# A pre-norm graph network: the hand-over between layers in another order, and one norm named later

## The chip, the cores and the metric

The program runs on one core of a Trainium2 chip, in one launch. The metric is the device time of that core in microseconds (us). A core has a matrix engine (TensorE, PE; weight loads are listed as PEld), VectorE (DVE), ScalarE (ACT), GpSimd (POOL) and SyncE (SP), which issues most DMAs. Each engine works through its own queue in order and waits on semaphores for the others.

## What is computed

```python
mu, var = jnp.mean(x, 0), jnp.var(x, 0)          # x: relu of a layernorm of the input
h = (x - mu) * rsqrt(var + EPS) * bn_w + bn_b
h = _gcn(h, src, dst, gcn_in_w, gcn_in_b, n)
for i in range(L):
    a = _attn(_ln(h, ln2_w[i], ln2_b[i]), cond, Wq[i], Wk[i], Wv[i], Wo[i])
    h = h + a
    u = _ln(h, ln3_w[i], ln3_b[i]) @ geglu_w[i] + geglu_b[i]
    val, gate = jnp.split(u, 2, axis=-1)
    f = val * jax.nn.gelu(gate, approximate=False)
    h = h + f @ ffo_w[i] + ffo_b[i]
h = _gcn(h, src, dst, gcn_out_w, gcn_out_b, n)
```

There are N = 1024 rows of D = 512, L = 4 layers, 8 heads of 64. `_gcn` multiplies by a weight and sums over 16384 edges. `_attn` is cross attention: 16 batches of 64 rows look at 256 rows of `cond` each, with k = cond @ Wk and v = cond @ Wv. All is float32.

## The kernel before

The rows `h` stay in SBUF as eight blocks of 128 (`h[0]` to `h[7]`, views of `hall`). Attention runs over eight groups g, one for each block of 128 rows (two batches). While group g is weighted, k and v of group g + 1 are made.

k and v are made with float32 products of higher precision than one pass gives: each operand is split into three parts. `left_parts` splits a group's condition `ct` into `ah` (ACT), `al` (DVE) and `as` (POOL, from `ah` and `al`); `right_parts` splits a weight into `bh` (ACT), `bl` and `bs` (DVE). A `Twelve` is one 128x512 block of k or v: `begin` multiplies the first two pairs of parts (two groups of four matmuls) and has ACT scale the bank in place; `end` adds the third pair (one group) and copies the bank out, on ACT or DVE by the flag `by`. `staggered` runs a list of such units so that a unit's `end` comes after the next one's `begin`, and runs other work `beside` a unit.

Weights are multiplied in seven products instead of eight (a Strassen form), hence names such as `wqs`, `ln2S` (sums of blocks), and `ffn_out` with products 0, 6, 4, 5, 1, 3, 2 into the four banks `fa` to `fd`; DVE adds them to `kept` and `hall`. `ffn_out(l, r, s, ...)` does half s of the rows (blocks 0, 1, 4, 5 or 2, 3, 6, 7). Its argument `beside` holds up to three functions: the third is called after the first add of `kept`, the first after the three shared adds, the second after the add of product 1.

What sets the order: the engine queues are filled by a planner that simulates the program and issues, on each engine, whatever is ready and was named first. `pin` keeps an instruction behind everything named before it on its engine, `in_order(engine)` does that for a whole block, `issue_after` and `waiting_for` hold instructions behind a given one. Most matmuls are pinned. Tiles come from pools: `slots` has 36 slots of 128x1024 floats, from which weights, parts, `kT`, `v` and `lnT` all come; `work` has ten tiles of 128x512 (`xn`, `pr`, `pT`, `oT` and others); PSUM has eight banks.

The hand-over from layer l to l + 1 is the end of the loop over layers, in one block with DVE in written order. It names the loads of Wk, condition 0, Wv, Wq, the bias row and condition 1 (`load_projections`), then: the first half of the last `ffn_out`, with Wk's split beside it; the moments of blocks 0, 1, 4, 5; the second half, with, in this order, those blocks' root and norm on ACT (`ready_first`, `scaled_by_act`), condition's parts (`split_cond`) and Wv's parts; the moments, root and norm of the other four blocks. The next layer begins with `keys` and `values` of group 0, eight units, with `turn_first` (transposes of the normalised blocks into `lnT`, scaled by ACT and DVE) beside unit 4 and unit 7; then the queries.

In group 6 (`NG - 2`) the norm of blocks 4 and 5 (`ln3_norm`: moments and root as small operations on 128x2, and two scalings, all on DVE) is named ahead of group 7's keys, and POOL makes the sums of the geglu weights (`geglu_weights`, held behind the scores). `mix` transposes the probabilities, copies them (`pT`, on ACT and DVE in turn), and weights v with them (bank `po`). The output projection of two groups at a time is a generator, `attn_out_pair`, whose last step is one product and its adds.

Of the kernel before, what the change touches and what calls it, by code (L numbers as in the profile page):

```python
# [8 lines left out]
F32 = mybir.dt.float32  # L9
# [16 lines left out]
def gnn_kernel(  # L26
# [85 lines left out]
    def t512(name, dtype=F32):  # L112
        return work.tile([P, 512], dtype, tag="t512", name=name)
# [27 lines left out]
    def rsqrt(var, name, eps=0.0):  # L141


        k = var.shape[1]

        def t(n, dtype=F32):
            return small.tile([P, k], dtype, tag=f"rs_{n}{k}", name=f"{n}_{name}",
                              bufs=4 if k == 1 else 2)

        v = t("v")  # L150
        rsqrt.first = nc.vector.tensor_scalar(v, var, float(eps), None, OP.add)
        y = t("y")
        nc.vector.tensor_scalar(y.bitcast(I32), v.bitcast(I32), -0.5, RSQRT_SEED, OP.mult, OP.add)
        for i in range(3):
            a = t("a")
            nc.vector.scalar_tensor_tensor(a, y, -0.5, v, OP.mult, OP.mult)
# [14 lines left out]
    def deviations(mv, name):  # L171

        return rsqrt(mv.rearrange("p (n c) -> p n c", c=2)[:, :, 1], name, EPS)
# [100 lines left out]
    def load_cond(l, g):  # L274
        if g < NG:
            raw_x[l, g] = slots_of(2, f"ct_{l}_{g}")
            for k in range(2):
                nc.sync.dma_start(raw_x[l, g][k].rearrange("p a b -> p (a b)"),
                                  cond_dram[g][:, 1024 * k:1024 * (k + 1)])
# [72 lines left out]
    class Twelve:  # L352
# [22 lines left out]
        def end(self):  # L375
            self.multiply(2, False, True)
            if self.by:
                nc.vector.tensor_copy(self.to, self.bank)
            else:
                nc.scalar.copy(self.to, self.bank)  # L380

    def staggered(units, beside):

# [14 lines left out]
    def values(l, g, wv, begun=None, n=0):  # L398

        vs[g] = begun or slots_of(2, f"v_{l}_{g}")  # L400
        return [Twelve(f"v_{l}_{g}_{c}", conds[g], c, wv, vs[g][c // 2][:, c % 2, :], c % 2)
                for c in range(n, 2 * MB)]

    kTs, vs = {}, {}
# [107 lines left out]
    bst = small.tile([P, KC, 2, 6], F32, tag="bst", name="bst", bufs=1)  # L512
# [817 lines left out]
    def scaled_by_act(blocks, mv, root, name):  # L1330

        n = len(blocks)
        less = small.tile([P, 4], F32, tag="less", name=f"less_{name}", bufs=1)[:, :n]
        scaled_by_act.last = nc.vector.scalar_tensor_tensor(less, mv.rearrange("p (n c) -> p n c", c=2)[:, :, 0], -1.0,
                                       root, OP.mult, OP.mult)
        for i, nb in enumerate(blocks):
            xns[nb] = t512(f"xn_{name}_{nb}")
            nc.scalar.activation(xns[nb], h[nb], AF.Identity, bias=less[:, i:i + 1],
                                 scale=root[:, i:i + 1])

    mv_ready = {}

    def take_moments(l, blocks):
        n = len(blocks)
# [24 lines left out]
    def four_wide(name):  # L1369
        return wos.tile([P, 4, 512], F32, tag="wos", name=name)  # L1370


    def load_projections(l):
        raw = [load_w(Wk[l], f"wk_{l}")]
        load_cond(l, 0)
        raw.append(load_w(Wv[l], f"wv_{l}"))
        raw.append(load_w(Wq[l], f"wq_{l}"))
        raw.append(load_row(ffo_b, l * D, f"ffb_{l}"))
        load_cond(l, 1)
        return raw  # L1380

    def load_last():
        w = load_w(gcn_out_w, "w_out")
# [18 lines left out]
            nc.sync.dma_start(c_dram[:, :, d, :].rearrange("s p n -> p s n"), by_sources(C[d]))  # L1402
    for l in range(L):

        lnS = ln_sums(l)
        if l:
            units = keys(l, 0, wk) + values(l, 0, wv)
            to_turn = [0, 1, 4, 5], [2, 3, 6, 7]
        else:
            scale_first(1, deviations(mv_first[1], "ln2_0_4"))  # L1410
            with waiting_for(scale_first.last, mybir.EngineType.Pool):
                wq = weight_sums(wq, "wqs_0")
            units = keys(0, 0, wk, begun["k0"], 2) + values(0, 0, wv, begun["v0"], 1)
# [74 lines left out]
        def scale_kept():  # L1488

            root = deviations(mv_kept, f"ln3_{l}_0")  # L1490
            scaled_by_act(range(4), mv_kept, root, f"ln3_{l}")

        def nothing():
            pass
# [2 lines left out]
        for g in range(NG - 1):  # L1497
# [4 lines left out]
            for end in ends:  # L1502
                end()
            if g == NG - 2:
                ln3_norm(g - 2, g - 1)
            if g == NG - 2:
                with waiting_for(scores.last, mybir.EngineType.Pool):
                    left = geglu_weights(l, 0, *raw)
            if not g:
# [1 line left out]
                    wo7 = wo_sums(wo)  # L1511
            if g in (1, 2):
                fetch_x(2 * l + g - 1)
            k = keys(l, g + 1, wk, *((begun["k1"], 1) if l == 0 and g == 0 else ()))
            for i, u in enumerate(k):
                u.begin()
                if i > 1:
# [186 lines left out]
        if last:  # L1704
            w_out, base, again, dinv_row = load_last()
            with waiting_for(Gated.last, mybir.EngineType.Pool):
                w_out = out_weights(nc.gpsimd, L, 0, w_out)
            ffn_out(l, R - 1, 0, fT, wff, kept)
        else:
            lnT = [slots_of(2, f"ln2T_{l + 1}_{i}") for i in range(2)]  # L1710
            raw_wk, raw_wv, wq, ffb = load_projections(l + 1)
            wk, wv = [[], [], []], [[], [], []]

            def split(to, raw, name, *of):
                for i in of:
                    for part, t in zip(to, right_parts(raw[i:i + 1], f"{name}_{l + 1}_{i}")):
                        part.extend(t)
# [157 lines left out]
```

## Time and profile before

| what | value |
|---|---|
| time, median of 3 runs | 2452.02 us (2450.74 to 2453.26) |
| the profiled execution | 2452.32 us, span 2450.5 us |
| busy: PE, PEld | 97%, 73% |
| busy: DVE, ACT, POOL | 66%, 41%, 38% |
| mean granted TensorE clock | 0.994 |

The span is the time from the first to the last instruction; the rest of the execution's time lies around it. Busy shares are means over stages of different kinds: where PE is busy for nearly the whole of a stage, the other engines' idle time there costs nothing, so the list of PE's waits and the stages in which they lie say more. A row of the timeline reads: start, duration, engine, line, operation, output from inputs, shapes, how many merged, and in brackets the idle time before it and what ended it.

### The profile page before, as it was taken

To read this page: it belongs to the slowest core of one execution; us is meant where nothing else is said; L and a number is where in the kernel's file an instruction comes from. 1 tells how busy PE (TensorE), PEld (TensorE's weight loads), DVE (VectorE), ACT (ScalarE), POOL (GpSimd) and SP (SyncE) were. 2 spreads that over 40 slices of the span, in tenths; PEclk is the share of its full clock that TensorE was granted. 3 is DMA by queue.
4 is the path that set the end of the run, shared out by engine and by line. 5 is a ranking of instruction groups with operands and counts; after the bars stand their busy time and mean duration, and the time that the engine had idled before them with its cause. 6 is when DMAs were issued, how large, how long until landed. Compare 5 with 4: busy or idle time off the path is not lost. (4 is left out here: it accounts for less than half of the span.)

```text
span 2450.5 us, 33701 instructions
## 1 busy us (share of the span) xinstructions
PE 2374.2 (97%) x12528; PEld 1777.1 (73%) x12528; DVE 1606.8 (66%) x3028; ACT 992.8 (41%) x2011; POOL 937.2 (38%) x839
## 2 busy tenths in 40 slices
PE   8999999999999999999989999999999999999999
PEld 5668885677757886577776887577776887567787
DVE  9865456787764456877775445777785445678764
ACT  7444443343244444343334443533334444434320
POOL 0142233565133223565422223455523223356531
PEclk9999999999999999999999999999999999999999
DMA  6142110111301110021302101011121111011140
GB/s 197 37 133 83 64 57 18 44 43 52 108 26 66 39 48 23 22 61 47 116 1 65 65 19 52 9 52 52 43 91 48 48 53 35 18 45 42 52 146 35
DMA packets 108843, 138.31 MB, mean 56 GB/s; under 512 B 8232, under 2 KB 65904, under 8 KB 108672
## 3 DMA queue, kind: packets, MB, share of 16 engines
q1 hardware_dynamic: 106576, 130.64, 16.6%
q0 software_dynamic: 1376, 4.30, 0.5%
q8 instruction: 104, 1.70, 0.3%
q10 hardware_dynamic: 720, 1.11, 0.1%
q14 instruction: 67, 0.55, 0.1%
HBM read 119.25 MB, written 16.78 MB: 56 GB/s over the span
## 5 line engine op out<-in xcount | busy, mean ns | idle before, releaser
L316 POOL TENSOR_TENSOR as_c<-ah_c,al_c 128x512 fp32r<-128x512 f32 x128 | 189.4, 1507 | 243.4 <-DVE al_c L314 237.4
L1112 ACT ACTIVATE g<-g 128x512 f32<-128x512 f32 x192 | 112.1, 584 | 280.8 <-PE g L1098 278.5
L373 ACT ACTIVATE v<-v 128x512 f32<-128x512 f32 x127 | 74.0, 583 | 256.7 <-PE v L362 256.7
L1049 POOL TENSOR_TENSOR gsa<-gha,gla 128x512 fp32r<-128x512 f32 x96 | 125.7, 1331 | 104.2 <-DVE gla L1046 104.2
L362 PE MATMUL v<-bh_wv,ah_c 128*128 128x512 f32 x508 | 149.5, 417 | 5.7 <-ACT kT L380 5.7
L1049 POOL TENSOR_TENSOR gsb<-ghb,glb 128x512 fp32r<-128x512 f32 x48 | 70.0, 1458 | 219.4 <-DVE glb L1046 219.4
L833 ACT ACTIVATE pr<-sc,nmax 128x256 f32<-128x256 f32 x256 | 118.3, 475 | 68.4 <-DVE nmax L828 68.4
L362 PE MATMUL v<-bs_wv,as_c 128*128 128x512 f32 x508 | 143.9, 405 | 0.0
L362 PE MATMUL k<-as_c,bs_wk 128*128 128x512 f32 x500 | 135.8, 400 | 7.2 <-POOL as_c L316 7.0
L362 PE MATMUL v<-bl_wv,al_c 128*128 128x512 f32 x508 | 138.2, 394 | 0.0
L362 PE MATMUL k<-al_c,bl_wk 128*128 128x512 f32 x500 | 135.9, 393 | 1.2 <-DVE al_c L314 1.2
L1098 PE MATMUL g<-gr,gsa 128*128 128x512 f32 x384 | 136.6, 437 | 0.0
L362 PE MATMUL k<-ah_c,bh_wk 128*128 128x512 f32 x500 | 136.4, 395 | 0.0
L1125 ACT ACTIVATE g<-g,gcols 128x512 f32<-128x512 f32 x96 | 67.5, 703 | 164.4 <-DVE g L1133 161.2
L1213 PE MATMUL fa<-wff,fT 128*128 128x256 f32 x512 | 122.2, 381 | 11.8 <-DVE kept L1223 11.8
L905 POOL TENSOR_TENSOR os<-oT 128x256 f32<-128x256 f32 x12 | 8.8, 734 | 318.8 <-DVE oT L879 318.8
L373 ACT ACTIVATE k<-k 128x512 f32<-128x512 f32 x125 | 72.2, 585 | 132.5 <-PE k L362 132.5
L1098 PE MATMUL g<-gr,gha 128*128 128x512 f32 x384 | 122.8, 401 | 0.0
L1213 PEld LDWEIGHTS fa<-wff,fT 128*128 128x128 f32 x512 | 96.3, 190 | 33.0 <-DVE kept L1223 16.2
L1098 PE MATMUL g<-gl,gla 128*128 128x512 f32 x384 | 118.6, 390 | 0.0
L362 PEld LDWEIGHTS v<-bs_wv,as_c 128*128 128x128 f32 x508 | 94.2, 189 | 25.9 <-issue 6.2
L362 PEld LDWEIGHTS k<-as_c,bs_wk 128*128 128x128 f32 x500 | 92.4, 189 | 27.9 <-POOL as_c L316 10.3
(368 smaller groups left out, 5888.1 us busy)
## 6 DMA issues: line engine op xcount, KB each, us to landing
ct<-cond_dram SPq DMA_DIRECT2D x48, 512.0 KB, 4.2
wff<-in_L_gnn_ffo_w_dram SPq DMA_DIRECT2D x32, 512.0 KB, 4.3
gxb<-in_L_gnn_geglu_w_dram SPq DMA_DIRECT2D x96, 128.0 KB, 2.2
gxa<-in_L_gnn_geglu_w_dram SPq DMA_DIRECT2D x96, 128.0 KB, 2.3
cond<-in_L_gnn_cond_dram SPq DMA_DIRECT2D x32, 256.0 KB, 3.7
cond_dram<-ct SPq DMA_DIRECT2D x16, 512.0 KB, 3.7
wk<-in_L_gnn_Wk_dram SPq DMA_DIRECT2D x8, 512.0 KB, 6.1
wv<-in_L_gnn_Wv_dram SPq DMA_DIRECT2D x8, 512.0 KB, 8.4
```

Of the source, the lines that this page charges most:

```text
L316: nc.gpsimd.tensor_tensor(twelve_bits(s)[:, k, :], h[:, k, :], l[:, k, :], OP.subtract)
L362: pin(nc.tensor.matmul(self.bank, twelve_bits(left[k // 2])[:, k % 2, self.c * P:(self.c + 1) * P], twelve_bits(right[k // 2])[:, k % 2, : ...
L373: nc.scalar.mul(self.bank, self.bank, 1.0 + TINY)
L833: nc.scalar.activation(pr3[:, a, :], ps3[:, a, :], AF.Exp, bias=nmax[:, a:a + 1], accum_out=tot[:, a:a + 1])
L905: t.tensor_tensor(s1, a21, a22, OP.add)
L1049: pin(nc.gpsimd.tensor_tensor(s_at, h_at, l_at, OP.subtract))
L1098: pin(nc.tensor.matmul(to, self.part(i, which)[:, k, :], self.rights[i][which].bitcast(F32R)[:, k, :], start=start and k == 0, stop=stop a ...
L1112: pin(nc.scalar.mul(to, to, 1.0 + TINY))
L1125: pin(nc.scalar.activation(to, of, AF.Gelu, bias=gcols[:, cg:cg + 1]))
L1213: each(nc.tensor.matmul(to[:, q * M:(q + 1) * M], left[i][k][:, (2 * s + q) * P:(2 * s + q + 1) * P], right[i][:, k, :], start=start and q ...
```

## The change

- `load_projections` is gone. Wk, condition 0 and Wv are loaded ahead of the last `ffn_out`; Wq, the bias row and condition 1 are named after it.
- In the second half of that `ffn_out`, condition's parts come first, right after the add of `kept`, then the moments of the first four blocks; their root comes after the shared adds. Wv's parts come after `ffn_out`, ahead of the other blocks' moments.
- The norms themselves (`scaled_by_act`) are returned as functions and run in the next layer, beside units 1 and 5.
- In the eight units of group 0 of layers 1 to 3, ACT is held to the written order and copies every block out (`by=(0, 0)`).
- Wq's sums are named after the first half's sums.
- `kT`, `v`, `lnT` and `lnS` get their slots when they are first written or needed (`blocks_in`).
- The pair of blocks 4 and 5 leaves its last step to the next group, as the other pairs do, and the norm of blocks 4 and 5 is named behind `mix`.

```diff
-    def keys(l, g, wk, begun=None, n=0):
-
-        kTs[g] = begun or slots_of(2, f"kT_{l}_{g}")
-        return [Twelve(f"k_{l}_{g}_{c}", wk, c, conds[g], kTs[g][c // 2][:, c % 2, :], c % 2)
-                for c in range(n, KC)]
+    def blocks_in(kept, g, name):
+
+        def block(c):
+            def to():
+                if g not in kept:
+                    kept[g] = slots_of(2, name)
+                return kept[g][c // 2][:, c % 2, :]
+            return to
+
+        return block
+
+    def keys(l, g, wk, n=0, by=(0, 1)):
+
+        to = blocks_in(kTs, g, f"kT_{l}_{g}")
+        return [Twelve(f"k_{l}_{g}_{c}", wk, c, conds[g], to(c), by[c % 2]) for c in range(n, KC)]
...
     def ready_first(l, blocks):
         mv, name = mv_ready.pop(blocks[0]), f"ln2_{l}_{blocks[0]}"
-        scaled_by_act(blocks, mv, deviations(mv, name), name)
+        to_scale.append(scaled_by_act(blocks, mv, deviations(mv, name), name))
...
         if l:
-            units = keys(l, 0, wk) + values(l, 0, wv)
+            units = keys(l, 0, wk, by=(0, 0)) + values(l, 0, wv, by=(0, 0))
...
         def turn_some():
+            nonlocal lnT, wq
+            if l:
+                lnT = [slots_of(2, f"ln2T_{l}_{i}") for i in range(2)]
             turn_first(l, to_turn[0])
+            lnS.extend(ln_sums(l))
             if l:
                 sum_first(nc.gpsimd, 0)
                 sum_first(nc.gpsimd, 1)
-
-        staggered(units, {4 if l else 2: turn_some, len(units) - 1: lambda: turn_first(l, to_turn[1])})
+                with waiting_for(scaled_by_act.last, mybir.EngineType.Pool):
+                    wq = weight_sums(wq, f"wqs_{l}")
+
+        beside = {len(units) - 1: lambda: turn_first(l, to_turn[1])}
+        if l:
+            beside.update({1: to_scale.pop(0), 4: turn_some, 5: to_scale.pop(0)})
+            with in_order(mybir.EngineType.Activation):
+                staggered(units, beside)
+        else:
+            staggered(units, {2: turn_some, **beside})
...
-            if g == NG - 2:
-                ln3_norm(g - 2, g - 1)
             if g == NG - 2:
                 with waiting_for(scores.last, mybir.EngineType.Pool):
                     left = geglu_weights(l, 0, *raw)
...
             oTs.append(mix(l, g, probs, vs.pop(g), (k[-1].end, nothing, v[0].begin)))
+            if g == NG - 2:
+                ln3_norm(g - 2, g - 1)
...
             if g % 2:
                 next(pair)
+                ends.insert(0, lambda pair=pair: next(pair, None))
                 if g == NG - 3:
-                    next(pair, None)
                     scale_kept()
-                else:
-                    ends.insert(0, lambda pair=pair: next(pair, None))
...
-            lnT = [slots_of(2, f"ln2T_{l + 1}_{i}") for i in range(2)]
-            raw_wk, raw_wv, wq, ffb = load_projections(l + 1)
...
+            raw_wk = load_w(Wk[l + 1], f"wk_{l + 1}")
+            load_cond(l + 1, 0)
+            raw_wv = load_w(Wv[l + 1], f"wv_{l + 1}")
...
+            def condition_and_moments():
+                split_cond(l + 1, 0)
+                take_moments(l + 1, half[0])
 
             half = [0, 1, 4, 5], [2, 3, 6, 7]
             with in_order(mybir.EngineType.DVE):
-                ffn_out(l, R - 1, 0, fT, wff, kept, pin, (lambda: split(wk, raw_wk, "wk", 0),
-                                                          lambda: split(wk, raw_wk, "wk", 1)))
-                take_moments(l + 1, half[0])
-                ffn_out(l, R - 1, 1, fT, wff, kept, pin, (lambda: split_cond(l + 1, 0),
-                                                          lambda: split(wv, raw_wv, "wv", 0, 1),
-                                                          lambda: ready_first(l + 1, half[0])))
+                ffn_out(l, R - 1, 0, fT, wff, kept, pin, (lambda: split_wk(0), lambda: split_wk(1)))
+                ffn_out(l, R - 1, 1, fT, wff, kept, pin, (lambda: ready_first(l + 1, half[0]),
+                                                          lambda: None, condition_and_moments))
+                wq = load_w(Wq[l + 1], f"wq_{l + 1}")
+                ffb = load_row(ffo_b, (l + 1) * D, f"ffb_{l + 1}")
+                load_cond(l + 1, 1)
+                wv = right_parts(raw_wv, f"wv_{l + 1}")
                 take_moments(l + 1, half[1])
                 ready_first(l + 1, half[1])
-            with waiting_for(scaled_by_act.last, mybir.EngineType.Pool):
-                wq = weight_sums(wq, f"wqs_{l + 1}")
```

Beside these, `values` changes as `keys` does, `Twelve.end` calls `self.to()`, the root's tile `y` gets four buffers and `less` two, and `bst` of the first stage comes from another pool.

More of the change, by code (lines that the diff above doesn't have):

```diff
@@ L147, in t @@
             return small.tile([P, k], dtype, tag=f"rs_{n}{k}", name=f"{n}_{name}",
-                              bufs=4 if k == 1 else 2)
+                              bufs=4 if k == 1 or n == "y" else 2)
         v = t("v")
@@ L377, in end @@
             if self.by:
-                nc.vector.tensor_copy(self.to, self.bank)
+                nc.vector.tensor_copy(self.to(), self.bank)
             else:
-                nc.scalar.copy(self.to, self.bank)
+                nc.scalar.copy(self.to(), self.bank)
     def staggered(units, beside):
@@ L511, in gnn_kernel @@
     bmv = small.tile([P, KC, 2], F32, tag="bmv", name="bmv", bufs=1)
-    bst = small.tile([P, KC, 2, 6], F32, tag="bst", name="bst", bufs=1)
+    bst = gp.tile([P, KC, 2, 6], F32, name="bst")
     for i in range(2):
@@ L1332, in scaled_by_act, with scale @@
         n = len(blocks)
-        less = small.tile([P, 4], F32, tag="less", name=f"less_{name}", bufs=1)[:, :n]
+        less = small.tile([P, 4], F32, tag="less", name=f"less_{name}", bufs=2)[:, :n]
         scaled_by_act.last = nc.vector.scalar_tensor_tensor(less, mv.rearrange("p (n c) -> p n c", c=2)[:, :, 0], -1.0,
                                        root, OP.mult, OP.mult)
[L1336 to L1341, printed above, removed]
+        def scale():
+            for i, nb in enumerate(blocks):
+                xns[nb] = t512(f"xn_{name}_{nb}")
+                nc.scalar.activation(xns[nb], h[nb], AF.Identity, bias=less[:, i:i + 1],
+                                     scale=root[:, i:i + 1])
+        return scale
+    mv_ready, to_scale = {}, []
     def take_moments(l, blocks):
@@ L1370, in four_wide @@
         return wos.tile([P, 4, 512], F32, tag="wos", name=name)
[L1373 to L1380, printed above, removed]
     def load_last():
@@ L1412, in gnn_kernel @@
                 wq = weight_sums(wq, "wqs_0")
-            units = keys(0, 0, wk, begun["k0"], 2) + values(0, 0, wv, begun["v0"], 1)
+            kTs[0], vs[0], kTs[1] = (begun[n] for n in ("k0", "v0", "k1"))
+            units = keys(0, 0, wk, 2) + values(0, 0, wv, 1)
             to_turn = [0, 1, 2, 3], [4, 5, 6, 7]
         def turn_some():
+            nonlocal lnT, wq
+            if l:
+                lnT = [slots_of(2, f"ln2T_{l}_{i}") for i in range(2)]
             turn_first(l, to_turn[0])
+            lnS.extend(ln_sums(l))
             if l:
@@ L1490, in scale_kept @@
             root = deviations(mv_kept, f"ln3_{l}_0")
-            scaled_by_act(range(4), mv_kept, root, f"ln3_{l}")
+            scaled_by_act(range(4), mv_kept, root, f"ln3_{l}")()
         def nothing():
@@ L1513, in gnn_kernel @@
                 fetch_x(2 * l + g - 1)
-            k = keys(l, g + 1, wk, *((begun["k1"], 1) if l == 0 and g == 0 else ()))
+            k = keys(l, g + 1, wk, 1 if l == 0 and g == 0 else 0)
             for i, u in enumerate(k):
@@ L1709, in gnn_kernel, with split_wk @@
         else:
-            lnT = [slots_of(2, f"ln2T_{l + 1}_{i}") for i in range(2)]
-            raw_wk, raw_wv, wq, ffb = load_projections(l + 1)
[L1712 to L1717, printed above, removed]
+            raw_wk = load_w(Wk[l + 1], f"wk_{l + 1}")
+            load_cond(l + 1, 0)
+            raw_wv = load_w(Wv[l + 1], f"wv_{l + 1}")
+            wk = [[], [], []]
+            def split_wk(i):
+                for part, t in zip(wk, right_parts(raw_wk[i:i + 1], f"wk_{l + 1}_{i}")):
+                    part.extend(t)
+            def condition_and_moments():
+                split_cond(l + 1, 0)
+                take_moments(l + 1, half[0])
             half = [0, 1, 4, 5], [2, 3, 6, 7]
             with in_order(mybir.EngineType.DVE):
-                ffn_out(l, R - 1, 0, fT, wff, kept, pin, (lambda: split(wk, raw_wk, "wk", 0),
-                                                          lambda: split(wk, raw_wk, "wk", 1)))
-                take_moments(l + 1, half[0])
-                ffn_out(l, R - 1, 1, fT, wff, kept, pin, (lambda: split_cond(l + 1, 0),
-                                                          lambda: split(wv, raw_wv, "wv", 0, 1),
-                                                          lambda: ready_first(l + 1, half[0])))
+                ffn_out(l, R - 1, 0, fT, wff, kept, pin, (lambda: split_wk(0), lambda: split_wk(1)))
[5 more added lines that the diff above has]
+                wv = right_parts(raw_wv, f"wv_{l + 1}")
                 take_moments(l + 1, half[1])
                 ready_first(l + 1, half[1])
-            with waiting_for(scaled_by_act.last, mybir.EngineType.Pool):
-                wq = weight_sums(wq, f"wqs_{l + 1}")
     hs_out = [rows_of("hs_high_out"), rows_of("hs_low_out")]
```

8 lines of the change are left out of this document (4 added, 4 removed).

## The prediction

> **What bounds the kernel.** The page first, for which engine sets the time.
>
> ```profile
> span 2450.5 us, 33701 instructions
> PE 2374.2 (97%) x12528; PEld 1777.1 (73%) x12528; DVE 1606.8 (66%) x3028; ACT 992.8 (41%) x2011; POOL 937.2 (38%) x839
> ```
>
> TensorE (PE) is busy for 97% of the span, so only what it waits for can be won. Next the list of PE's waits: engine, line and tile, what it waited for, total us, times, longest us.
>
> ```profile
> PE po L856 <- DVE pT L870: 19.4, 4, 4.9
> PE fa L1213 <- DVE kept L1223: 11.8, 11, 1.7
> PE k L362 <- POOL as_c L316: 7.0, 6, 1.2
> PE v L362 <- ACT kT L380: 5.7, 3, 2.2
> ...
> PE ocd L296 <- DVE hall L937: 2.4, 4, 0.6
> ```
>
> Two places hold these waits. `po` waits once per layer for 4.85 us (19.4 / 4), inside the attention of group 6; `ocd` 0.6 us once per layer just ahead of it. `fa`, `k` and `v` wait where one layer hands over to the next, three times. The windows price both, with the lost clock; columns are window, its length, busy us (and instructions) of PE, PEld, DVE, ACT, POOL, the granted clock, DMA.
>
> ```profile
> 666.25:715.43 49.18, 42.50 (x185) 33.56 (x184) 37.99 (x81) 20.20 (x36) 17.97 (x16) 0.93 0.00 0
> 1237.57:1287.38 49.81, 41.49 (x186) 32.62 (x184) 37.90 (x81) 20.41 (x36) 17.93 (x16) 0.97 0.00 0
> 1810.50:1858.68 48.18, 39.88 (x185) 31.48 (x183) 37.88 (x81) 20.29 (x36) 17.95 (x16) 1.00 0.00 0
> 376.24:382.00 5.76, 5.76 (x43) 4.44 (x45) 1.14 (x2) 0.06 (x1) 0.00 (x0) 0.52 0.00 0
> 689.65:695.40 5.75, 5.75 (x14) 4.49 (x15) 5.54 (x10) 0.58 (x1) 0.00 (x0) 0.50 0.00 0
> ...
> 1847.50:1852.90 5.40, 5.40 (x24) 4.43 (x25) 2.98 (x8) 4.82 (x12) 4.53 (x6) 1.00 0.00 0
> ```
>
> The first three rows run from the first product of the second half of a layer's last ffn_out to the first product of the next layer's queries: 49.18, 49.81 and 48.18 us, 147.2 us together. PE's work in such a hand-over comes from its own timeline.
>
> ```profile
> 1810.50 1.89 PE L1213 MATMUL fa<-wff,fT 128*128 128x256 f32 x8
> 1812.22 1.89 PE L1213 MATMUL fc<-wff,fT 128*128 128x256 f32 x8
> ...
> 1819.27 1.99 PE L1213 MATMUL fa<-wff,fT 128*128 128x256 f32 x8 [1.70 <-DVE kept L1223]
> 1822.11 1.99 PE L1213 MATMUL fc<-wffs,fT 128*128 128x256 f32 x8 [0.85 <-DVE hall L1219]
> ...
> 1836.99 1.07 PE L362 MATMUL k<-ah_c,bh_wk 128*128 128x512 f32 x4
> 1837.90 1.07 PE L362 MATMUL k<-al_c,bl_wk 128*128 128x512 f32 x4
> ...
> 1855.84 1.91 PE L201 MATMUL tr_ln<-ident,xn_ln 128*128 128x128 f32 x16
> 1857.51 1.17 PE L362 MATMUL v<-bs_wv,as_c 128*128 128x512 f32 x4
> ```
>
> A product of ffn_out takes 1.73 us from start to start (1810.50 to 1812.22), a group of four matmuls of `k` or `v` 0.91, sixteen transposes 1.67. A hand-over holds 7 products, 8 units of 3 groups, 2 times 16 transposes: 12.1 + 21.8 + 3.3 = 37.2 us. So 147.2 - 111.6 = 35.6 us are lost in three, part of it as waits and part by the clock: after the waits for `as_c` the clock was 0.50 for 5.75 us.
>
> Why PE waits there, VectorE's (DVE) timeline says; its order is written by hand.
>
> ```profile
> 1815.35 0.69 DVE L168 BATCH_NORM_STATS2 st_ln<-hall 128x6 f32<-128x512 f32 x1
> ...
> 1818.56 0.66 DVE L1223 TENSOR_TENSOR kept<-fa,kept 128x512 f32<-128x512 f32 x1
> 1819.13 0.16 DVE L151 TENSOR_SCALAR v_ln<-mv 128x4 f32<-128x4 f32 x1
> ...
> 1821.38 0.68 DVE L1219 TENSOR_TENSOR hall<-fc,hall 128x512 f32<-128x512 f32 x1
> ...
> 1823.48 1.89 DVE L1219 TENSOR_TENSOR hall<-kept,hall 128x512 f32<-128x512 f32 x3
> 1825.30 2.35 DVE L314 SCALAR_TENSOR_TENSOR al_c<-ah_c,ct 128x1024 fp32r<-128x1024 f32 x2
> ...
> 1835.70 0.68 DVE L327 SCALAR_TENSOR_TENSOR bl_wv<-wv,bh_wv 128x512 fp32r<-128x512 f32 x1
> ```
>
> It runs without a gap: four moments (3.21 us, 1815.35 to 1818.56), `kept`, eleven small operations of a root and `less` (2.25 us, 1819.13 to 1821.38), adds, and only at 1825.30 condition's low parts `al_c`, when PE already wants them. GpSimd (POOL) then makes `as_c` against DVE's splitting of Wv, and much later Wq's sums:
>
> ```profile
> 1826.66 7.18 POOL L316 TENSOR_TENSOR as_c<-ah_c,al_c 128x512 fp32r<-128x512 f32 x4 [37.53 <-DVE al_c L314]
> ...
> 1844.10 1.27 POOL L238 TENSOR_TENSOR wqs<-wq,wq 128x512 f32<-128x512 f32 x1 [10.26 <-DVE less_ln L1334]
> ```
>
> **The hand-over, part by part.** I run the third one again in the new order. The add of `kept` no longer stands behind the moments: 1815.35 to 1816.0, and PE's fifth product starts at 1810.50 + 4 x 1.73 = 1817.4 with no wait (1.70 gone). Behind it now stand `al_c` (2.35), then the moments (3.21): 1821.6. The add `hall<-fc` ends at 1822.3, against 1822.06 before: the root has gone behind it, `al_c` has come ahead, nearly equal in price. PE has ended its fifth product at 1819.1 and waits 3.1 us in one piece, where it waited 1.70 + 0.85. So ffn_out itself ends 0.2 us later. The gain is in what follows: `al_c` is there at 1818.4 and `as_c` by about 1824 (from 1818.4, four at no more than the row's 7.18 / 4 end at 1825.6), and PE's first `k` begins at 1825.7, its first third part 3.6 later, so the waits for `al_c` and `as_c` are gone.
>
> DVE goes on: the other adds and the shared add of `kept` to 1825.4, root and `less` 2.25 to 1827.7, three adds 2.0 to 1829.7, Wv's split 8 x 0.68 = 5.4 to 1835.1, moments 3.2 to 1838.3, root 2.25 to 1840.6. PE, unhindered, wants Wv's low parts in its thirteenth group: 1825.7 + 12 x 0.91 = 1836.6. The cover is 1.5 us; each us beyond it costs PE one.
>
> ScalarE (ACT) gets a written order, and all eight copies instead of four.
>
> ```profile
> L373 ACT ACTIVATE v<-v 128x512 f32<-128x512 f32 x127 | 74.0, 583 | 256.7 <-PE v L362 256.7
> 1844.05 2.93 ACT L1338 ACTIVATE xn_ln<-hall,less_ln,y_ln 128x512 f32<-128x512 f32 x4 [1.75 <-DVE less_ln L1334]
> 1857.82 1.51 ACT L800 ACTIVATE ln2T<-tr_ln,cols 128x128 f32<-128x128 f32 x4
> ```
>
> Its work in the eight units: 8 scalings of 0.58, 8 copies of about the same, 2 times 2.93 for the norms, 16 turns of 0.38 (1.51 / 4): 21.3 us, in 25.1 of PE (21.8 + 3.3). The tightest places are u2's and u6's end: u2's scaling stands behind four norms and ends about 9.0 us after the first `k`, PE wants it at 9.1; I allow 0.4 us for both. The `v` unit that waited for ACT's copies of `kT` waits no more, since those copies stand ahead of the second four norms. Those need `less` at 1840.6 and stand in ACT's order at 1825.7 + 18.4 = 1844.1.
>
> On POOL Wq's sums come to stand beside the first half's sums: four of 1.27 and eight of half that width, estimated at half that time, 10 us from about 1841, wanted behind the first four query products, 1850.8 + 4 x 1.73 = 1857.7. Cover 6 us; DVE's own last sums can meet them there, up to 1.5 us in the bounds. On SP the loads of Wq, ffb and the second condition are named behind ffn_out, when SP has nothing else to issue; the planner may still issue them early, and late they would only touch Wq's sums. Slots named at first use free lnT's four, kT's and v's during ffn_out, which can only let the parts start earlier: nothing. Layer 0 keeps its order. The changed counts of `y` and `less` and the place of `bst` add no instruction: nothing.
>
> Sum: 12.1 + 3.1 + 21.8 + 3.3 + 0.4 = 40.7 us. The new 3.1 us wait can cost clock, which no row shows for that length. After a wait of 2.2 us (the longest of `v`) the clock stayed 1.00 (row from 1847.50); after 4.85 us it was 0.52 for 5.76 us, 2.8 us lost. 3.1 us lies between and nearer the lower; but two waits for `as_c` of 1.2 us close together brought 0.50 for 5.75 us, so I take 2.0 of the 0 to 2.9. Hand-over: 42.7; three: 128.1; gain 147.2 - 128.1 = 19.1 us, bounds 12 (2.9 of clock and 1.5 of further waits in each) and 25 (no clock lost).
>
> The Trainium skill ("TensorE: Matmul & The Clock Gate", HAM oscillation) wants idle gaps beyond about 3.4 us before the clock halves. By that rule the 3.1 us would cost nothing and the gain would be 25. The row from 689.65, after waits of 1.2 us, disagrees here.
>
> **The norms in group 6.** Today the norm of rows 4 and 5 sits on DVE ahead of the copies of `kT` and `pT`, beside POOL's sums of the geglu weights.
>
> ```profile
> 355.49 0.42 DVE L941 TENSOR_TENSOR hall<-ocd,hall 128x256 f32<-128x256 f32 x1 [1.28 <-PE ocd L296]
> ...
> 363.70 2.40 POOL L238 TENSOR_TENSOR ges<-wgate,wgate 128x1024 f32<-128x1024 f32 x1 [6.98 <-DVE v_ln L151]
> ...
> 363.88 2.24 DVE L156 SCALAR_TENSOR_TENSOR a_ln<-y_ln,v_ln 128x2 f32<-128x2 f32 x1
> ...
> 373.98 1.00 DVE L189 TENSOR_SCALAR xn_ln<-hall,mv_ln,y_ln 128x512 f32<-128x512 f32 x2
> ```
>
> A 128x2 operation takes 2.24 us there, as long as POOL's, four times in the chain; that is `po`'s wait. The change names the norm behind the weighting, but nothing pins it: neither `in_order` nor `issue_after` holds it. The planner takes what is ready:
>
> ```profile
> 1311.69 1.96 PE L821 MATMUL sc<-kT,qT 64*64 64x256 f32 x32
> ...
> 1312.56 0.69 DVE L1482 TENSOR_TENSOR x_again<-x_again,bias_out 128x512 f32<-128x512 f32 x1
> ```
>
> L1482 is named in group 1, behind its weighting, and runs at group 0's scores. DVE is free between the scores and the first `kT` copy, so I expect the chain there again, against the same four POOL operations. What moves for sure: the pair's last product goes behind the scores, so its wait of 0.6 is gone; scores come 1.5 us earlier (that wait, and the product's four matmuls at half of 1.73). DVE gets 0.42 + 0.69 of add and moments in between, so the chain starts 0.4 earlier and PE is 0.6 earlier: `po`'s wait grows by 0.2. The two scalings (1.00) may fall behind the copies, since their targets come from the pool of `pT`: 0 to 1.0 us. 0.6 - 0.2 + 0.5 = 0.9, times 4: 3.6 us, bounds 1.6 and 5.6.
>
> The Trainium skill ("SBUF — State Buffer", Who interferes with whom) says that a DVE instruction with two SBUF inputs is locked out by a reading GpSimd instruction until that one ends. The trace agrees: 2.24 beside 2.40 us.
>
> **Rivals.** First: the norms do land behind the weighting. For: the code names them so, and their target tiles share a pool with `pT`. Against: the rows above. Then `po`'s 4.85 us and 2.8 us of clock go too: 4 x (0.6 + 4.85 + 2.8) = 33; with 19.1, 52 us: 2400.
> Second: ACT's written order is the bound: a norm waiting for `less` at its head stops the scalings behind it, and PE. For: one queue, 21.3 of 25.1 us. Against: `less` is 3.3 us early or more (1827.7 for 1831.0, 1840.6 for 1844.1). It decides from there on; 7.6 us in each hand-over eat all 22.7 of the sum below: 2452.
> Third, slower: slots in the attention groups. `v` of the next group now gets its two slots only behind the six of the next condition's parts and the two of a load, which wait for slots themselves:
>
> ```profile
> 722.87 12.16 SPq L278 DMA_DIRECT2D ct<-cond_dram  x2
> ```
>
> Two issues took 12.16 us, the second waiting. If `v`'s copies come late beyond what spare PSUM banks cover, PE stops in up to 28 groups. From (22.7 + 4.9) / 28 = 1.0 us per group the kernel is slower; at 1.5 us it gives 2452 + 42 - 22.7 = 2471. Against: PE has no wait for such a slot now, and eight banks are there.
>
> **How the numbers follow.** 19.1 + 3.6 = 22.7 us. The profiled execution took 2452.32 us (span 2450.5), the median of the runs is 2452.02; from the latter 2429.3. Chances: forecast 0.58 (its own range 2421 to 2438, from 25.1 + 5.6 and 12 + 1.6 us; of it 0.15 for a clock that stays full, 25.1 + 3.6 us, 2423.3), norms behind 0.22, ACT 0.07, slots 0.13. A measurement tells 0.2% (4.9 us). Faster 0.80, same 0.07, slower 0.13. The range 2398 to 2448 holds the forecast, most of the first rival (its clock lost or not) and a part of the second.
>
> **What would show it.** Right: `k` waits for neither `as_c` nor `al_c`, `v` not for `kT`; `fc` waits 3.1 us; hand-overs of 41 to 43 us; `po` still waits about 4 us with 128x2 operations of 2.2 us. Wrong: L168 and L151 of rows 4 and 5 behind `oT` in group 6 (first rival), PE waiting for ACT's scalings (second), `v` or `k` waiting for copies in the groups (third).

## The result and the profile after

The changed kernel takes 2434.72 us (median of 4 runs, 2432.47 to 2437.04) against 2451.38 us before (4 runs, 2450.18 to 2453.26): ratio 0.9931, 95% interval 0.9914 to 0.9949, so 16.7 us faster by the medians. The profiled executions differ by 19.9 us (spans 2450.5 and 2430.6); the sums below are of these two. The total comes near the forecast, and its parts do not: the hand-over gave a third of what was forecast, group 6 almost four times as much.

First the changed page and its list of PE's waits, in the columns of the prediction.

```profile
span 2430.6 us, 33690 instructions
PE 2367.9 (97%) x12528; PEld 1776.1 (73%) x12528; DVE 1596.9 (66%) x3016; ACT 999.5 (41%) x2023; POOL 940.0 (39%) x839
...
PE po L866 <- DVE pT L880: 12.4, 4, 3.1
PE qb L296 <- DVE ln2S L233: 8.1, 3, 2.7
PE fc L1223 <- DVE hall L1229: 7.9, 3, 2.7
...
PE v L362 <- ACT v L373: 2.4, 3, 0.8
```

The waits of `k` for `as_c` and `al_c`, and of `v` and `tr_ln` for copies of `kT`, are gone. `po` waits 3.1 us, not 4.9. `fc` waits 2.65 us three times (0.85 before; forecast). New is `qb`, 2.7 us three times, for sums of the turned rows `ln2S` (in no list of the prediction). The windows say what each place is worth: first the three hand-overs, as the prediction cut them, then from there (first query product) to the first scores.

```profile
661.20:704.76 43.56, 40.03 (x186) 32.77 (x184) 32.44 (x78) 19.80 (x37) 15.36 (x16) 0.96 0.00 1
1227.36:1271.01 43.65, 40.11 (x185) 32.78 (x183) 32.45 (x78) 19.81 (x37) 15.35 (x16) 0.96 0.00 1
1793.49:1837.16 43.67, 40.13 (x185) 32.81 (x183) 32.45 (x78) 19.81 (x37) 15.35 (x16) 0.96 0.00 1
704.76:732.01 27.25, 24.55 (x57) 10.39 (x57) 16.35 (x26) 5.84 (x12) 8.35 (x5) 1.00 0.27 96
1271.01:1298.29 27.28, 24.55 (x57) 10.39 (x57) 16.36 (x26) 6.02 (x12) 8.38 (x5) 1.00 0.28 97
1837.16:1865.90 28.74, 26.02 (x56) 11.02 (x57) 16.38 (x26) 5.98 (x12) 8.38 (x5) 0.94 0.29 92
```

The same queries of before, the third of them:

```profile
1858.68:1883.00 24.32, 24.32 (x57) 10.48 (x57) 13.37 (x27) 5.26 (x11) 5.03 (x4) 1.00 0.34 109
```

Up to the first query product a hand-over takes 43.6 us; the three took 147.2 and take 130.9: 16.3 us won. The queries behind it took 24.3 us each and take 27.3, 27.3 and 28.7: 10.3 us given back. Six are left.

The timelines of ScalarE and VectorE show why the queries wait: the second half's turns of before (the first query product starts at 1858.68),

```profile
1857.82 1.51 ACT L800 ACTIVATE ln2T<-tr_ln,cols 128x128 f32<-128x128 f32 x4
...
1860.98 1.04 DVE L798 TENSOR_SCALAR ln2T<-tr_ln,cols 128x128 f32<-128x128 f32 x3
...
1863.95 0.41 DVE L233 TENSOR_TENSOR ln2S<-ln2T,ln2S 128x256 f32<-128x256 f32 x1
```

and of after (it starts at 1837.16), with GpSimd's parts of the next condition:

```profile
1836.45 1.53 DVE L314 SCALAR_TENSOR_TENSOR al_c<-ah_c,ct 128x1024 fp32r<-128x1024 f32 x1 [0.53 <-ACT ah_c L313]
1838.54 1.64 DVE L314 SCALAR_TENSOR_TENSOR al_c<-ah_c,ct 128x1024 fp32r<-128x1024 f32 x1
1838.65 0.81 ACT L810 ACTIVATE ln2T<-tr_ln,cols 128x128 f32<-128x128 f32 x2 [0.60 <-DVE ln2T L808]
1839.06 6.48 POOL L316 TENSOR_TENSOR as_c<-ah_c,al_c 128x512 fp32r<-128x512 f32 x4
1840.87 0.81 ACT L810 ACTIVATE ln2T<-tr_ln,cols 128x128 f32<-128x128 f32 x2 [0.24 <-DVE ln2T L808]
1842.93 1.49 DVE L233 TENSOR_TENSOR ln2S<-ln2T,ln2S 128x256 f32<-128x256 f32 x1
1844.34 0.40 DVE L808 TENSOR_SCALAR ln2T<-tr_ln,cols 128x128 f32<-128x128 f32 x1
...
1846.53 0.42 DVE L233 TENSOR_TENSOR ln2S<-ln2T,ln2S 128x256 f32<-128x256 f32 x1
```

A block's four transposes lie in one bank; ScalarE turns the even quarters, VectorE the odd ones, and on a bank each waits for the other. Before, ScalarE takes four turns in a row, of several banks, and VectorE its own four and three behind them: all are turned 3.3 us after the first query product. In the written order ScalarE takes the two quarters of one bank one after the other. Then each of its pairs stands behind a turn of VectorE (0.60 and 0.24 us idle ahead of the second and the third), and VectorE has the low parts of the next condition (1.53 and 1.64 us) in between: the last turn ends 7.6 us after the first query product. The sum that `qb` waits for ends at 1846.95, and `qb` wants it at 1844.4.

The turns aren't all of it. Counted from the first query product, that sum ends 4.1 us later than before (9.8 us for 5.7). VectorE's eight sums take 5.9 us here and 3.3 us before: the first four now run beside GpSimd's `as_c` (the L233 at 1842.93 takes 1.49 us, the one at 1846.53, behind `as_c`, 0.42). Before, the first half of `as_c` was made ahead of the sums; now GpSimd is at Wq's sums until 1839.1, where another edit of the change put them.

The Trainium skill ("PSUM — Partial Sum Buffer", PSUM bank collisions raise a hardware error) says that two engines may not touch one bank at the same partitions at once, reads included, and that software has to keep them apart; the trace agrees, with waits of a quarter to 0.6 us on the other engine's turn; no run here shows what an overlap would do.

In group 6 the norm of rows 4 and 5 was hoisted again, as forecast: VectorE's chain in layer 1, and `po` behind it.

```profile
927.83 1.11 DVE L151 TENSOR_SCALAR v_ln<-mv_ln 128x2 f32<-128x2 f32 x1
929.18 2.24 DVE L156 SCALAR_TENSOR_TENSOR a_ln<-y_ln,v_ln 128x2 f32<-128x2 f32 x1
931.45 2.30 DVE L158 TENSOR_TENSOR b_ln<-a_ln,y_ln 128x2 f32<-128x2 f32 x1
933.98 2.21 DVE L156 SCALAR_TENSOR_TENSOR a_ln<-y_ln,v_ln 128x2 f32<-128x2 f32 x1
938.43 1.77 PE L866 MATMUL po<-pT,v 128*64 128x64 f32 x30 [3.11 <-DVE pT L880]
```

Windows from group 6's scores to group 7's, layers 0 and 1, of after,

```profile
353.79:389.01 35.22, 32.11 (x237) 26.28 (x237) 24.89 (x50) 15.23 (x39) 11.01 (x6) 1.00 0.08 31
918.44:955.18 36.74, 33.63 (x237) 27.54 (x236) 24.89 (x50) 15.22 (x39) 11.01 (x6) 0.95 0.08 30
```

and of before:

```profile
355.38:393.98 38.60, 33.77 (x233) 27.36 (x232) 25.08 (x49) 15.14 (x39) 10.21 (x5) 0.91 0.09 28
927.79:965.27 37.48, 32.62 (x233) 26.75 (x232) 25.09 (x49) 15.14 (x39) 10.22 (x5) 0.95 0.09 30
```

Over four layers (table below) they sum to 145.4 us against 151.9, 6.5 won. The scores themselves start 1.70 us earlier in each layer, 6.8 in four: together 13.3 us.

### The profile page after: what moved, and what is told of

Same layout as the page of the kernel before. It is cut to its first block, busy times and chain, and to the rows that moved or that the text cites. A ratio compares the mean times of both kernels' runs of the same rounds, so it can differ in the third digit from the quotient of the medians.

```text
span 2430.6 us, 33690 instructions
## 1 busy us (share of the span) xinstructions
PE 2367.9 (97%) x12528; PEld 1776.1 (73%) x12528; DVE 1596.9 (66%) x3016; ACT 999.5 (41%) x2023; POOL 940.0 (39%) x839
## 3 DMA queue, kind: packets, MB, share of 16 engines
q10 hardware_dynamic: 720, 1.11, 0.1%
## 5 line engine op out<-in xcount | busy, mean ns | idle before, releaser
L314 DVE SCALAR_TENSOR_TENSOR al_c<-ah_c,ct 128x1024 fp32r<-128x1024 f32 x64 | 92.2, 1445 | 33.0 <-ACT ah_c L313 33.0
```

Source lines behind the costliest of these rows:

```text
L314: nc.vector.scalar_tensor_tensor(twelve_bits(l), h, -1.0 / TINY, x, OP.mult, OP.add)
```

## The experiments

One table of all runs first; the last two columns are windows cut as above, in us. Each time is the median of its runs; the kernel before ran beside them with 2453.53 us (first four) and 2454.02 us (last four).

| kernel | us | ratio to before, 95% interval | three hand-overs, three queries | group 6, by layer |
|---|---|---|---|---|
| before | 2451.4 | 1 | 147.2, 72.9 | 38.6, 37.5, 38.2, 37.6 |
| changed | 2434.7 | 0.9931 (0.9914 to 0.9949) | 130.9, 83.3 | 35.2, 36.7, 36.8, 36.6 |
| handover_only | 2448.0 | 0.9981 (0.9972 to 0.9991) | 131.0, 84.9 | 38.5, 37.9, 38.3, 37.9 |
| turns_free | 2421.0 | 0.9868 (0.9852 to 0.9885) | 126.5, 75.4 | 36.7, 36.8, 35.2, 36.7 |
| norm_pinned | 2412.6 | 0.9838 (0.9822 to 0.9855) | 129.1, 83.4 | 31.8 in all |
| moments_late | 2443.4 | 0.9957 (0.9941 to 0.9974) | 138.8, 86.1 | 36.8 in all |
| no_act_order | 2427.4 | 0.9893 (0.9877 to 0.9910) | 130.4, 75.6 | 36.8, 36.7, 38.0, 36.7 |
| ges_late | 2413.9 | 0.9834 (0.9818 to 0.9851) | 130.0, 85.1 | 31.8 in all |
| combo | 2399.9 | 0.9781 (0.9765 to 0.9798) | 123.8, 76.2 | 31.8 in all |
| combo_split | 2398.2 | 0.9776 (0.9760 to 0.9793) | 121.7, 76.5 | 31.8 in all |

**handover_only: the hand-over's edits alone.**

```diff
+            if g == NG - 2:
+                ln3_norm(g - 2, g - 1)
...
-                ends.insert(0, lambda pair=pair: next(pair, None))
                 if g == NG - 3:
+                    next(pair, None)
                     scale_kept()
+                else:
+                    ends.insert(0, lambda pair=pair: next(pair, None))
```

> The changed kernel with its edits of group 6 taken back (the norm of rows 4 and 5 named ahead of the keys again, the pair's last product ahead of the scores), so that the hand-over's edits stand alone. My theory from the two traces: the hand-overs give 16.3 us up to the first query product and hand back 10.3 us inside the queries, where the second query product now waits 2.7 us for the sums of the turned rows; they bring about 6.5 us net and group 6 brings 13.3. Then this kernel takes about 2445 us (2443 to 2447), po waits 4.85 us again. The rival, the sizes of the prediction (hand-over 19.1, group 6 3.6): 2433 us.

5.6 us below before by the medians, where 6.5 were expected, and far from the prediction's 19.1. In its trace `po` waits 4.9 us four times and `qb` 2.7 us three times. So two thirds of what the change brings come from group 6.

**turns_free: the turns out of ScalarE's written order.**

```diff
     def in_order(engine):
...
-            if i.engine == engine:
+            if i.engine == engine and i.name not in free:
...
-                nc.scalar.activation(to, of, AF.Identity, bias=b, scale=w)
+                free.add(nc.scalar.activation(to, of, AF.Identity, bias=b, scale=w).ins.name)
```

> The changed kernel, with ScalarE's sixteen turns of a hand-over (ln2T from tr_ln) left out of its written order; scalings, copies and norms stay in it. Theory A: the written order takes the two turns of one bank one after the other, each behind VectorE's turn of the same bank, and VectorE has the next condition's low parts in between; so the turns end 7.5 us after the first query product and the sums 10 us after it. With the turns free ScalarE goes on with another bank, the turns end about 2 to 4 us earlier and the wait of the second query product (2.7 us, three times, with 1.5 us of clock once) goes to below 1 us: 2426 us (2424 to 2429). Theory B: the wait comes from GpSimd's sums of Wq, which share VectorE's port, or from the low parts alone; then the wait stays above 2 us and the time at 2433 to 2435.

Theory A, and 5 us more than it. In PE's waits `qb` is gone and a short one stands there:

```profile
PE qa L296 <- DVE ln2T L808: 1.2, 3, 0.4
```

In the timelines, ScalarE's eight turns of the first half, and VectorE's first sums of the second:

```profile
1816.73 3.39 ACT L810 ACTIVATE ln2T<-tr_ln,cols 128x128 f32<-128x128 f32 x8
...
1830.77 2.85 DVE L231 TENSOR_TENSOR ln2S<-ln2T,ln2T 128x256 f32<-128x256 f32 x2
```

The first eight turns take 3.39 us in one piece; in the changed kernel they took from 1823.61 to 1828.93, and `v`'s scaling, behind them and four norms, came late (`v` waited 0.80 us for it). That wait is gone too: a hand-over takes 42.2 us. Something of theory B is left, with another neighbour: two of VectorE's sums take 2.85 us beside GpSimd's `as_c`, which runs from 1830.65 to 1833.3 (0.75 before), and the queries take 25.1 us for 24.3. The sum that `qb` needs now ends 7.4 us after the first query product. So of the 4.1 us by which it came later in the changed kernel, the order of the turns made 2.3; the other 1.8 fit the meeting with `as_c`, which no run moved.

**norm_pinned: the norm really behind the weighting.**

```diff
-        nc.vector.tensor_copy(oT, po)
+        mix.last = nc.vector.tensor_copy(oT, po)
...
-                ln3_norm(g - 2, g - 1)
+                ln3_norm(g - 2, g - 1, behind=mix.last)
```

> The changed kernel with the norm of rows 4 and 5 in group 6 bound behind the copy of oT, which ends the weighting; nothing else differs on any engine. Theory A (the first rival of the prediction, made true): the chain of 128x2 operations no longer stands ahead of the copies of kT and pT and no longer meets GpSimd's four sums of geglu's weights; they take 0.16 to 0.2 us each, po's wait of 3.1 us goes in all four layers, and with it the clock lost behind it in three of them (1.5 us each): 12.4 + 4.6 = 17 us, 2418 us (2415 to 2423). Theory B: the chain, the moments and two scalings (about 5 us) behind oT come too late for the transposes of rows 4 and 5 (9.3 us behind oT's copy in the changed kernel) or delay the copies of v, and a wait for them takes po's place: 2428 to 2435 us.

Theory A, and 5 us more. From the timelines, one of the operations that took 2.2 us, the two scalings, and PE's transposes of rows 4 and 5:

```profile
938.18 0.16 DVE L156 SCALAR_TENSOR_TENSOR a_ln<-y_ln,v_ln 128x2 f32<-128x2 f32 x1
...
939.94 1.00 DVE L189 TENSOR_SCALAR xn_ln<-hall,mv_ln,y_ln 128x512 f32<-128x512 f32 x2
...
945.58 1.03 PE L201 MATMUL tr_ln<-ident,xn_ln 128*128 128x128 f32 x8
```

and the window from scores to scores:

```profile
914.76:946.55 31.79, 31.79 (x238) 26.10 (x237) 18.15 (x50) 15.25 (x39) 11.01 (x6) 1.00 0.11 35
```

Everything is done at 940.9 and wanted at 945.6. PE is busy for all of the 31.79 us at a clock of 1.00: no wait is left in group 6.

**ges_late: which of the two, place or neighbour.**

```diff
-            if g == NG - 2:
-                with waiting_for(scores.last, mybir.EngineType.Pool):
-                    left = geglu_weights(l, 0, *raw)
...
             oTs.append(mix(l, g, probs, vs.pop(g), (k[-1].end, nothing, v[0].begin)))
+            if g == NG - 2:
+                with waiting_for(mix.last, mybir.EngineType.Pool):
+                    left = geglu_weights(l, 0, *raw)
```

> The changed kernel with GpSimd's sums of geglu's weights in group 6 moved behind the weighting (bound to the copy of oT); the norm of rows 4 and 5 stays ahead of the copies of kT and pT. Theory A: it is only the meeting with those sums that makes the chain of 128x2 operations long (three of 2.2 to 2.3 us and one of 1.1 us where 0.16 are needed, 7.2 us); without them the chain ends 7 us earlier, po's wait of 3.1 us goes though the norm is still in front: 2418 us (2414 to 2423), unless the late sums (four of 2.4 us, about 10 us) delay the products of geglu in group 7. Theory B: the norm's place, not GpSimd, is what counts: po still waits 2 us or more and the time stays at 2430 to 2435 us.

Theory A. The chain stands ahead of the copies as in the changed kernel, but GpSimd's sums no longer run beside it:

```profile
926.47 0.16 DVE L156 SCALAR_TENSOR_TENSOR a_ln<-y_ln,v_ln 128x2 f32<-128x2 f32 x1
...
938.15 3.07 DVE L189 TENSOR_SCALAR xn_ln<-hall,mv_ln,y_ln 128x512 f32<-128x512 f32 x2
```

The chain is over by 928.2, and VectorE then waits 1.54 us for `k` before it can copy `kT`. Group 6 takes 31.8 us, as with the norm behind. So it was the meeting with GpSimd that cost, not the norm's place; the scalings meet the sums now (3.07 us for 1.00) and delay nobody.

**moments_late: the wait of `fc` taken away.**

```diff
-            def condition_and_moments():
-                split_cond(l + 1, 0)
+            def moments_and_root():
                 take_moments(l + 1, half[0])
+                ready_first(l + 1, half[0])
...
-                ffn_out(l, R - 1, 1, fT, wff, kept, pin, (lambda: ready_first(l + 1, half[0]),
-                                                          lambda: None, condition_and_moments))
+                ffn_out(l, R - 1, 1, fT, wff, kept, pin, (moments_and_root, lambda: None,
+                                                          lambda: split_cond(l + 1, 0)))
```

> The changed kernel with the first half's moments moved from ahead of VectorE's add of fc to just ahead of its root; condition's parts stay where they are. Theory A: in each hand-over fc's wait of 2.65 us goes, and with it the clock that is lost behind it (granted 0.66 to 0.70 for 5.1 to 5.4 us, 1.7 us): 4.3 us three times, 13 us, 2421 us. Theory B: VectorE is full through the whole hand-over, so that what PE gains at fc it waits later, for Wv's low parts (about 1 us) and at the second query product, whose sums come no earlier: fc's wait is gone, the wait of qb grows from 2.7 to 5 us or more, and the time changes by less than 3 us: 2432 to 2437 us.

Neither: `fc`'s wait is gone, `qb` waits less (2.2 us), and the kernel is 8.7 us slower than the changed one. PE waits for ScalarE instead. Its waits:

```profile
PE v L362 <- ACT v L373: 11.6, 3, 3.9
...
PE k L362 <- ACT k L373: 4.9, 3, 1.7
```

and from the timelines VectorE's adds of `kept` and a pair of ScalarE's turns:

```profile
1812.77 4.26 DVE L1229 TENSOR_TENSOR hall<-kept,hall 128x512 f32<-128x512 f32 x3
...
1835.72 0.81 ACT L810 ACTIVATE ln2T<-tr_ln,cols 128x128 f32<-128x128 f32 x2 [4.27 <-DVE ln2T L808]
```

The adds of `kept` now run beside GpSimd's `as_c` and take 4.26 us for three (1.90 in the changed kernel, where the moments stood there). The root comes later, the norms wait 2.09 us for it at the head of ScalarE's order, and `k`'s scaling behind them; then a turn waits 4.27 us for VectorE's turn of the same bank, with `v`'s scaling behind it. The wait of `k` is the prediction's second rival, made to happen; that of `v`, the longer one, is again a turn.

**no_act_order: no written order at all.**

```diff
-            with in_order(mybir.EngineType.Activation):
-                staggered(units, beside)
+            staggered(units, beside)
```

> The changed kernel without ScalarE's written order in the hand-over; the copies stay with ScalarE and the norm of group 6 where the change puts it. Theory A: the order is needed for the scalings and copies and harmful for the turns only; without it the norms are taken between scalings (two of them ahead of the copies of kT), and k or v wait 1 to 2 us for ScalarE: between the changed kernel and the one with free turns, 2424 to 2430 us. Theory B: the order brings nothing at all; then as the kernel with free turns, 2421 us, or below.

Theory A: `qb`'s wait falls to 0.5 us, but `k` waits for ScalarE, 4.7 us in the three hand-overs. In the third ScalarE takes four norms and a part of Wv ahead of the first scalings, and `k` waits 2.7 us:

```profile
1810.63 2.93 ACT L1350 ACTIVATE xn_ln<-hall,less_ln,y_ln 128x512 f32<-128x512 f32 x4 [25.19 <-DVE less_ln L1344]
...
1815.13 1.16 PE L362 MATMUL k<-as_c,bs_wk 128*128 128x512 f32 x4 [2.69 <-ACT k L373]
```

Hand-overs and queries take 206.0 us together, 201.9 with the turns alone free, 214.2 in the changed kernel: the order over scalings, copies and norms is worth about 4 us, the order over the turns costs about 12.

**combo and combo_split: both repairs, and then `fc`.** The first joins the edits of turns_free and norm_pinned. The second also takes the moments of two rows in `behind[0]` and of the other two in `behind[1]`:

```diff
         product(6, c, True)
-        add(h22, c)
+        add(h22, c); behind[0]()
         product(4, d, True)
-        add(h22, d)
+        add(h22, d); behind[1]()
```

> The changed kernel with both repairs: ScalarE's turns of a hand-over out of its written order, and the norm of rows 4 and 5 bound behind the copy of oT. If the two places are independent (theory A), their gains against the changed kernel add: 2434.7 to 2421.0 is 13.7, to 2412.6 is 22.1, together 35.8: 2399 us (2396 to 2402). If one clock dip feeds the other or the planner moves something else (theory B), part is lost: 2404 us or more.

> As the kernel with both repairs, and in the hand-over the four moments stand two behind the first add of fc and two behind the first add of fd, where they still run beside GpSimd's as_c, instead of all four ahead of the first add of fc. Theory A: fc's wait of 2.65 us and the clock lost behind it (1.7 us) go, and since the adds of kept still run behind as_c and the root ends where it ended, nothing is late behind it: 3 x 4.3 = 13 us below the kernel with both repairs, 2386 us (2383 to 2391). Theory B, as the kernel with late moments showed: ScalarE's norms wait for a root that comes no earlier while TensorE is 4 us ahead, and k or v wait for scalings: the gain stays below 5 us.

The repairs add, to 2399.9 us, 1 us from the sum. The split does what it says and brings 1.7 us (2398.2): theory B. `fc` waits no more, and `v` waits instead, for a scaling that stands behind six turns of ScalarE, which stand behind VectorE:

```profile
1800.11 2.44 ACT L810 ACTIVATE ln2T<-tr_ln,cols 128x128 f32<-128x128 f32 x6 [3.34 <-DVE ln2T L808]
...
1803.09 1.19 PE L362 MATMUL v<-bs_wv,as_c 128*128 128x512 f32 x4 [1.38 <-ACT v L373]
```

VectorE, not PE, sets the pace there: its second `less` ends 29.5 us behind the second half's first product here and 29.7 in the changed kernel, so that PE, let go at `fc`, only reaches the next wait sooner. Most of the gain lies in the first hand-over (42.2 to 40.6 us), the only one of combo in which `fc`'s wait had cost clock; the other two gain 0.2 us each (40.8 to 40.6). combo_split is the fastest kernel here, 2.2% below before (ratio 0.9776, 0.9760 to 0.9793).

## Why the prediction was right, and where it was wrong

**The hand-over up to the queries.** Forecast 42.7 us, measured 43.6. The waits went as listed. `fc` waits 2.65 us (forecast 3.1), and from its start to the first key product now pass 4.95 to 5.06 us, where 3.37 passed before: 1.6 to 1.7 us of clock (forecast 2.0). `v` waits 0.80 us at u6 where 0.4 was allowed for both tight places. With these sizes the terms add up to 42.3 us; the other 1.3 are in no term and in no wait of the list (several groups of matmuls start 0.1 to 0.3 us late). That the clock term came near is partly luck: the row from 689.65, on which it rests in part, follows two waits of 1.17 us, and in the third hand-over of before, which was clocked at 1.00 throughout, PE waits the same twice.

**What failed: ScalarE's sum, and with it the second rival.** The working added 16 turns of 0.38 us as if ScalarE made them in one piece. The row they came from was taken from a kernel in which the planner chose their order. Written down, they alternate with VectorE's on each bank, so ScalarE waits for an engine that the sum of ScalarE's work doesn't contain. The second rival had the right engine and the wrong place: it looked for a norm at the head of the queue, and the stall was in the turns; it ate 10.3 us behind the window in which the working stopped. That the working stopped at the first query product was the second half of the error: its cover of 6 us was for Wq's sums, and it gave VectorE's own last sums up to 1.5 us, in the bounds alone, for meeting these. They met `as_c` instead and took 2.6 us more. With the turns freed the hand-over gives nearly what was forecast: in turns_free 147.2 + 72.9 - 126.5 - 75.4 = 18.2 us, for 19.1.

**Group 6: the mechanism right, the size not.** The chain was hoisted, 128x2 operations of 2.2 us stand there again, and the scores came 1.70 us earlier (forecast 1.5). Then two terms were mis-sized. The chain meets GpSimd's sums with three long operations and one of 1.11 us instead of four long ones: 7.9 us for 9.0. In the changed kernel these sums start 1.3 us ahead of the chain's L151 and before 0.2 us behind it; the forecast took the meeting as unchanged. And the scalings fell behind `oT` in every layer: 0.9 us, where the forecast took half. So `po`'s wait, by the forecast's terms 4.85 + 0.2 - 0.5 = 4.55 us, is 3.1. In layer 1, where the clock is alike, the scores come 1.70 us earlier and the window is 0.74 shorter: 2.4 us for 0.9. The rest is clock: in layer 0 it was 0.91 in the window before and 1.00 after, and the window is 3.4 us shorter where layer 1's is 0.74.

**The first rival** is the kernel norm_pinned: group 6 takes 31.8 us in each layer, 151.9 - 127.2 = 24.7 us less, and with scores that come 1.70 us earlier (6.8 in four) that is 31.5 us for the forecast's 33. Its price was nearly right; that nothing pins the norm was right too. **The third rival** is ruled out for this change: the list of waits holds none of `k`, and `v`'s three lie in the hand-overs, none in a group.

**The total** was near by luck, because two errors offset each other: 13 us too much in the hand-over, 10 too little in group 6; 0.6 of the 19.9 us lie elsewhere.

Left open: the slots named at first use were not tried by themselves, nor were the two edits of group 6 (the pair's last step and the norm's place in the text) apart from each other, nor `as_c` away from VectorE's last sums.

## What to carry to other kernels

A written order for one engine is also an order for every engine that shares something with it: before fixing it, ask of each pair of neighbours in the list whether the second waits for work of another engine that the first released (here the two quarters of one bank), and leave those out. A forecast's window has to run until the work of both versions is the same again, not until the last edit. And naming work later needn't move it in a planner that takes what is ready (here only the two scalings moved); bind it to the instruction that it is to follow, or move its neighbour.

## What the runs showed of the hardware

The same wait in the same place did and did not cost clock: `fc`'s 2.65 us in the three hand-overs of combo.

```profile
668.83:674.20 5.37, 5.25 (x17) 4.39 (x18) 4.88 (x17) 0.00 (x0) 1.09 (x1) 0.68 0.00 0
1226.70:1232.00 5.30, 5.16 (x23) 4.46 (x24) 4.82 (x16) 0.00 (x0) 1.11 (x1) 1.00 0.00 0
```

0.68 for 5.4 us in the first, 1.00 in the second, and in the third too. The prediction took the length of a wait to decide; at this length something that the trace doesn't show does. The Trainium skill ("TensorE: Matmul & The Clock Gate", What's actually happening) describes an activity window of about 3.4 us that runs free of the program, so that a change depends on where in it the work falls; that would fit, though here a wait shorter than such a window was enough, and no run shifted it on purpose.

The other: a VectorE operation of 128x2 elements costs 0.16 us alone and 2.2 us beside a GpSimd sum of 1024 columns, when it starts just behind the sum: it ends with it (in the prediction's rows at 366.12 and 366.10). Longer adds are slowed as well: three of 512 columns take 4.26 us beside `as_c`, 1.90 without.
